# Sums of absolute differences on half an image of one sample, with the quantised images passed once through DRAM

## The chip, the cores and the metric

The kernel runs on one core of one Trainium2 chip. The metric is the time of that core for one execution, in microseconds (us). Runs that are compared are fast ones, within 1.5% of the fastest of their kernel. Where only a single run exists, it is unknown whether it was a fast one, and the text says "in one run".

In this text PE is TensorE, DVE is VectorE, ACT is ScalarE, POOL is GpSimd and SP is SyncE. SP computes nothing here: it issues most of the transfers.

## The reference, cut to what matters

The network has four layers and an encoder and decoder on 16 samples of 32 channels of 128 x 128. Only the second layer (`_L1_conv`) is changed in earnest. It quantises the normalised image to whole numbers from -127 to 127, and for each of 32 filters sums |patch - weight| over 32 channels and 9 taps.

```python
def _ste_quant(x, scale):                  # value only
    return round(clip(x / scale, -127, 127))

def _adder2d(qx, qw):
    """out[n,f,i,j] = -sum_{c,kh,kw} |patch - w|"""
    patches = conv_general_dilated_patches(qx, (3, 3), (1, 1), [(1, 1), (1, 1)])
    ...
    def per_out(wk):
        return -sum(abs(pr - wk[None, :, None]), axis=1)

qx = _ste_quant(x, INPUT_SCALE)            # INPUT_SCALE = 2 ** -7
qw = _ste_quant(weight, s_w)               # s_w: a power of two from max |weight|
ys = _adder2d(qx, qw) * INPUT_SCALE
```

## The kernel before

The identity used is |q - w| = 2 max(q - w, 0) - q + w. DVE or ACT makes a **tile** d = max(q - w, 0) for one tap: in this kernel for one filter and four samples, in the changed one for four filters and one sample. PE multiplies the tile by a matrix of -1/64 that sums the channels into the output rows of PSUM. The term in q needs the same matmuls for every filter ("corrections", with 1/128), and the term in w is a constant (`sumw`).

In this form the 128 partitions are (channel, four samples), and a chunk is 32 rows of four samples. There are 16 chunks.

```python
R = 32
with tc.tile_pool(name="s1_ps", bufs=8, space=PSUM) as ps:
    for g in range(NG):                      # four groups of four samples
        for ch in range(H // R):             # four chunks of 32 rows
            xc = xp.tile([128, R + 2, W], F32, name="xc")
            nc.sync.dma_start(xc[:, off : off + n, :], cb_view(x1, g, lo, n))
            ...                              # quantise into qb; qa is its copy with borders
            nc.scalar.copy(qa[:, off : off + n, 1 : W + 1], qv)
            acc = [ps.tile([128, 512], F32, name="acc") for _ in range(8)]
            for tap in range(9):             # corrections: 288 matmuls
                for k in range(8):
                    for j in range(4):
                        nc.tensor.matmul(acc[k][32 * j : 32 * j + 32, :], sel16[:, 8, :],
                                         window(tap)[:, 4 * k : 4 * k + 4, :],
                                         start=tap == 0, stop=False)
            for f8 in range(8):
                for tap in range(9):
                    for j in range(4):       # j == 3 on ACT (2 buffers), others on DVE (6)
                        ...
                        nc.vector.tensor_scalar(d, window(tap), qw[:, i : i + 1], 0.0,
                                                ALU.subtract, ALU.max)
                    ...                      # 32 matmuls add the four tiles to acc
            for k in range(8):               # finishing
                nc.vector.scalar_tensor_tensor(v, acc[k], sumw, v, ALU.subtract, ALU.add)
                nc.vector.bn_stats(stat[:, g, 8 * ch + k, :], v)
            nc.scalar.dma_start(cb_view(x2, g, R * ch, R), xc[:, 1 : R + 1, :])
```

All eight buffers of the pool in PSUM (the banks, below) belong to one chunk, so the next chunk's corrections cannot begin before the last tile of this one: the last matmuls of the second chunk's tiles start at 1978.59 us, the corrections of the third at 1998.43.

Of the kernel before, what the change touches and what calls it, by code (L numbers as in the profile page):

```python
# [6 lines left out]
F32 = mybir.dt.float32  # L7
F16 = mybir.dt.float16
# [7 lines left out]
HW = H * W  # L16
CHW = C * HW
NG = 4
# [20 lines left out]
def cb_view(t, g, row0, nrows):  # L39

    return bass.AP(t.tensor, t.offset + g * 4 * CHW + row0 * W, [[HW, C], [CHW, 4], [1, nrows * W]])


# [28 lines left out]
def norm_stats(nc, pool, ps, mv, n, avg, eps):  # L72



    mean = pool.tile([128, n], F32, name="ns_mean")
    nc.vector.tensor_copy(mean, mv[:, :, 0])
    p1 = ps.tile([128, 512], F32, name="ps")
    nc.tensor.matmul(p1[:, :n], avg, mean, start=True, stop=True)
    m = pool.tile([128, n], F32, name="ns_m")  # L80
    nc.vector.tensor_copy(m, p1[:, :n])
    d = pool.tile([128, n], F32, name="ns_d")
    nc.vector.tensor_sub(d, mean, m)
    nc.vector.tensor_mul(d, d, d)
    nc.vector.tensor_add(d, d, mv[:, :, 1])
    p2 = ps.tile([128, 512], F32, name="ps")
    nc.tensor.matmul(p2[:, :n], avg, d, start=True, stop=True)
    v = pool.tile([128, n], F32, name="ns_v")
    nc.vector.tensor_copy(v, p2[:, :n])
    return m, inv_sqrt(nc, pool, v, n, eps)  # L90
# [10 lines left out]
def stage0(nc, tc, keep, cst, x, w0, b1, b2, x1):  # L101
# [3 lines left out]
    with ExitStack() as ctx:  # L105
# [104 lines left out]
        with tc.tile_pool(name="s0_ps2", bufs=2, space=PSUM) as ps:  # L210
            out = []
            for v in norm_stats(nc, sm, ps, mv, NG, cst["avg2_bc"], 1e-5):
                p = ps.tile([128, 512], F32, name="ps")
                nc.tensor.matmul(p[:, :NG], cst["bc_to_cb"], v, start=True, stop=True)
                out.append(keep.tile([128, NG], F32, name=f"s0_out{len(out)}"))
                nc.vector.tensor_copy(out[-1], p[:, :NG])
            return out


def stage1(nc, tc, keep, cst, sel16, m1, r1, x1, w, x2):  # L220
# [4 lines left out]
    R = 32  # L225
    with ExitStack() as ctx:
        sm = ctx.enter_context(tc.tile_pool(name="s1_sm", bufs=1))
        r128 = sm.tile([128, NG], F32, name="r128")
        nc.vector.tensor_scalar(r128, r1, 128.0, None, ALU.mult)


        qw = sm.tile([128, 288], F32, name="qw")
        nc.sync.dma_start(qw, bass.AP(w.tensor, w.offset, [[288, 32], [0, 4], [1, 288]]))
        top = sm.tile([128, 1], F32, name="top")
        nc.vector.tensor_reduce(top, qw, AX.X, ALU.max, apply_absolute_value=True)
        alltop = sm.tile([128, 1], F32, name="alltop")
        nc.gpsimd.partition_all_reduce(alltop, top, 128, bass_isa.ReduceOp.max)
        scale = sm.tile([128, 1], F32, name="scale")
        nc.vector.tensor_scalar(scale, alltop, 1.0 / 127.0, 1e-8, ALU.mult, ALU.max)
        nc.vector.tensor_scalar(scale, scale, 2.0**0.5, None, ALU.mult)  # L240
        nc.vector.tensor_scalar(scale.bitcast(I32), scale.bitcast(I32), 0x7F800000, None, ALU.bitwise_and)
        nc.vector.reciprocal(scale, scale)
        nc.vector.tensor_scalar(qw, qw, scale, -127.0, ALU.mult, ALU.max)
        nc.vector.tensor_scalar(qw, qw, 127.0, RND, ALU.min, ALU.add)
        nc.vector.tensor_scalar(qw, qw, RND, None, ALU.subtract)
        neg = sm.tile([128, 288], F32, name="neg")
        nc.vector.tensor_scalar(neg, qw, -1.0, None, ALU.mult)


        taps = sm.tile([128, 32], F32, name="taps")  # L250
        nc.vector.tensor_reduce(taps, qw.rearrange("p (f t) -> p f t", t=9), AX.X, ALU.add)
        tapb = sm.tile([128, 32, 4], F32, name="tapb")
        nc.vector.tensor_tensor(tapb, bcast(taps[:, :], 2, 4), bcast(cst["m4_cb"], 1, 32), ALU.mult)
        sumw = sm.tile([128, 1], F32, name="sumw")
        with tc.tile_pool(name="s1_ps0", bufs=1, space=PSUM) as ps:
            p = ps.tile([128, 512], F32, name="ps")
            nc.tensor.matmul(p[:, :1], tapb.rearrange("p f b -> p (f b)"), cst["ones"][:, :1], start=True, stop=True)
            nc.vector.tensor_scalar(sumw, p[:, :1], 2.0**-7, None, ALU.mult)

        stat = sm.tile([128, NG, 32, 6], F32, name="stat2")  # L260
        xp = ctx.enter_context(tc.tile_pool(name="s1_x", bufs=2))
        tp = ctx.enter_context(tc.tile_pool(name="s1_t", bufs=1))
        qp = ctx.enter_context(tc.tile_pool(name="s1_q", bufs=2))
        dp = ctx.enter_context(tc.tile_pool(name="s1_d", bufs=2))
        with tc.tile_pool(name="s1_ps", bufs=8, space=PSUM) as ps:
            for g in range(NG):
                for ch in range(H // R):
                    lo, hi = max(R * ch - 1, 0), min(R * ch + R + 1, H)
                    off = lo - (R * ch - 1)
                    n = hi - lo  # L270
                    xc = xp.tile([128, R + 2, W], F32, name="xc")
                    nc.sync.dma_start(xc[:, off : off + n, :], cb_view(x1, g, lo, n))


                    qa = qp.tile([128, R + 2, W + 2], F16, name="qa")
                    qb = qp.tile([128, R + 2, W], F16, name="qb")
                    t = tp.tile([128, R + 2, W], F32, name="t")
                    tv, qv = t[:, off : off + n, :], qb[:, off : off + n, :]
                    nc.vector.tensor_scalar(
                        tv, xc[:, off : off + n, :], m1[:, g : g + 1], r128[:, g : g + 1], ALU.subtract, ALU.mult  # L280
                    )
                    nc.vector.tensor_scalar(tv, tv, -127.0, 127.0, ALU.max, ALU.min)
                    nc.vector.tensor_scalar(qv, tv, RND, RND, ALU.add, ALU.subtract)
                    nc.scalar.copy(qa[:, off : off + n, 1 : W + 1], qv)
                    nc.gpsimd.memset(qa[:, :, 0], 0.0)
                    nc.gpsimd.memset(qa[:, :, W + 1], 0.0)
                    for edge, row in ((ch == 0, 0), (ch == H // R - 1, R + 1)):
                        if edge:
                            nc.gpsimd.memset(qa[:, row, :], 0.0)
                            nc.gpsimd.memset(qb[:, row, :], 0.0)  # L290

                    def window(tap):
                        kh, kw = tap // 3, tap % 3
                        return qb[:, kh : kh + R, :] if kw == 1 else qa[:, kh : kh + R, kw : kw + W]

                    acc = [ps.tile([128, 512], F32, name="acc") for _ in range(8)]
                    for tap in range(9):
                        for k in range(8):
                            for j in range(4):
                                nc.tensor.matmul(  # L300
                                    acc[k][32 * j : 32 * j + 32, :],
                                    sel16[:, 8, :],
                                    window(tap)[:, 4 * k : 4 * k + 4, :],
                                    start=tap == 0,
                                    stop=False,
                                )
                    for f8 in range(8):
                        for tap in range(9):
                            ds = []
                            for j in range(4):  # L310
                                i = 9 * (8 * j + f8) + tap
                                if j == 3:
                                    d = dp.tile([128, R, W], F16, name="d_act", bufs=2)
                                    nc.scalar.activation(d, window(tap), AF.Relu, bias=neg[:, i : i + 1])  # L314
                                else:
                                    d = dp.tile([128, R, W], F16, name="d_dve", bufs=6)
                                    nc.vector.tensor_scalar(  # L317
                                        d, window(tap), qw[:, i : i + 1], 0.0, ALU.subtract, ALU.max
                                    )
                                ds.append(d)  # L320
                            for k in range(8):
                                for j in range(4):
                                    nc.tensor.matmul(  # L323
                                        acc[k][32 * j : 32 * j + 32, :],
                                        sel16[:, f8, :],
                                        ds[j][:, 4 * k : 4 * k + 4, :],
                                        start=False,
                                        stop=f8 == 7 and tap == 8,
                                    )
                    for k in range(8):  # L330
# [830 lines left out]
```

## Time and profile before

| | before |
|---|---|
| time, median of 3 runs | 9255.92 us (9252.01 to 9258.56) |
| PE busy | 7875.1 us, 85% of the span |
| DVE busy | 6114.6 us, 66% |
| ACT busy | 5084.6 us, 55% |
| first and last DVE tile of the changed layer start at | 1432.0 us and 5943.0 us |

One more view of this kernel beside those that the prediction shows is the busy time of the engines in a stretch inside the layer. Its columns are: stretch, length, busy us (and instructions) of PE, PE's weight loads, DVE, ACT and POOL, granted clock (the share of full speed that the chip granted to PE), DMA share (the busy share of the 16 DMA engines), GB/s.

```profile
1520.00:5550.00 4030.00, 3852.39 (x36850) 1952.10 (x36850) 3926.91 (x3347) 3746.84 (x1040) 66.30 (x42) 0.99 0.04 16
```

DVE is busy for 97% of it, and the DMA engines stand nearly idle, at a share of 0.04.

### The profile page before, as it was taken

The page shows a single profiled execution, that of the slowest core. Times are in us where ns is not written, and L with a number is a line of the kernel's source. Part 1 is how long each engine was busy: PE and PEld are TensorE (multiplying, and loading weights), DVE is VectorE, ACT ScalarE, POOL GpSimd, SP SyncE. Part 2 cuts the span into 40 slices and gives each one's busy share as a digit, 9 for nine tenths or more (in the row PEclk, how much of TensorE's full clock was granted, in tenths as well). Part 3 has the DMA queues.
Part 4 walks back from the last instruction along what each step waited for, and adds up shares of the span by engine and source line. Part 5 has one row for each costly group of instructions (what it writes and reads, how often), then busy time and mean ns, then how long its engine had stood idle before and what let it go on. Part 6 is the DMA issues. An engine that isn't in the chain of part 4 may idle for free.

```text
span 9251.5 us, 253991 instructions
## 1 busy us (share of the span) xinstructions
PE 7875.1 (85%) x117746; PEld 5052.1 (55%) x117746; DVE 6114.6 (66%) x7543; ACT 5084.6 (55%) x3270; POOL 332.4 (4%) x529
## 2 busy tenths in 40 slices
PE   4999988999999999999999999794845968768955
PEld 3888874445444444544445544493734645545832
DVE  5444448999999999999999999830634233232233
ACT  1444437989989899998989989700000110101122
POOL 0111110000000000000000000000000000000000
PEclk9999998999999999999999999855555968778977
DMA  9799921000000000000000000242731111111067
GB/s 199 57 80 78 73 28 30 20 20 20 1 20 20 20 20 12 10 20 20 20 20 1 20 20 10 74 126 54 253 107 53 42 57 36 52 42 36 26 161 182
DMA packets 1503138, 494.74 MB, mean 53 GB/s; under 512 B 1416956, under 2 KB 1420540, under 8 KB 1486332
## 3 DMA queue, kind: packets, MB, share of 16 engines
q1 hardware_dynamic: 1460764, 365.54, 24.5%
q10 hardware_dynamic: 41312, 112.95, 3.7%
q8 instruction: 922, 15.11, 0.7%
q14 instruction: 140, 1.15, 0.0%
HBM read 331.12 MB, written 147.33 MB: 52 GB/s over the span
## 4 chain that ended last, share of the span: by engine, by line
DVE 41%; PE 38%; issue 15%; DMA 2%; SPq 2%; ACT 1%; DVEq 0%; ACTq 0%; POOL 0%; POOLq 0%
DVE d_dve L317 35%; PE acc L905 10%; PE pg L179 5%; PE pg L180 4%; PE acc L646 4%; PE acc L565 3%; PE pg L181 2%; PE acc L300 2%; PE p L379 2%; PE acc L793 2%; PE pf L479 1%; DVE xc L332 1%; PE acc L323 1%; DVE stat L333 1%; PE pa L459 1%
## 5 line engine op out<-in xcount | busy, mean ns | idle before, releaser
L323 PE MATMUL acc<-d_dve,sel 128*32 128x512 f16 x27648 | 3994.7, 379 | 43.7 <-DVE d_dve L317 43.3
L323 PEld LDWEIGHTS <-sel 128*32 128x32 f16 x36864 | 2057.5, 95 | 2042.1 <-issue 217.6
L314 ACT ACTIVATE d_act<-qa,neg 128x4096 f16<-128x4096 f16 x768 | 2803.3, 3697 | 131.4 <-PE acc L323 130.3
L317 DVE TENSOR_SCALAR d_dve<-qa,qw 128x4096 f16<-128x4096 f16 x2304 | 2788.5, 1279 | 110.6 <-PE acc L323 86.0
L323 PE MATMUL acc<-d_act,sel 128*32 128x512 f16 x9216 | 2181.2, 380 | 0.0
L314 ACT ACTIVATE d_act<-qb,neg 128x4096 f16<-128x4096 f16 x384 | 1419.4, 3696 | 0.0
L317 DVE TENSOR_SCALAR d_dve<-qb,qw 128x4096 f16<-128x4096 f16 x1152 | 1409.5, 1279 | 0.0
L905 PE MATMUL acc<-xp,fo_all 32*32 32x512 f32 x25600 | 934.9, 625 | 55.4 <-DVE pooled L806 48.8
L905 PEld LDWEIGHTS acc<-xp,fo_all 32*32 32x32 f32 x25600 | 658.4, 105 | 321.6 <-issue 161.6
L179 PE MATMUL pg<-h,bd 128*128 128x256 f32 x2048 | 652.2, 401 | 58.7 <-DVE h L199 58.4
L190 ACT ACTIVATE gt<-pg,bias 128x256 f32<-128x256 f32 x1024 | 400.9, 474 | 546.0 <-PE pg L181 545.8
L180 PE MATMUL pg<-h,bd 128*128 128x256 f32 x2048 | 622.8, 386 | 0.0
L817 ACT ACTIVATE y<-pooled,fo_b 32x128 f32<-32x128 f32 x256 | 102.4, 400 | 843.6 <-DVE pooled L806 840.2
L646 PE MATMUL acc<-xp 32*32 32x108 f32 x16384 | 326.1, 376 | 233.4 <-issue 228.3
L933 DVE TENSOR_TENSOR acc<-acc,cut 128x4 f32<-128x4 f32 x256 | 28.8, 166 | 700.4 <-PE acc L905 699.3
L181 PE MATMUL pg<-xn,bd 128*128 128x2 f32 (+62 forms) x2048 | 425.8, 289 | 9.4 <-DVE xn L163 9.4
L181 PEld LDWEIGHTS pg<-xn,bd 128*128 128x128 f32 x2048 | 396.6, 194 | 66.4 <-DVE xn L163 10.2
L180 PEld LDWEIGHTS pg<-h,bd 128*128 128x128 f32 x2048 | 398.2, 194 | 56.9
L646 PEld LDWEIGHTS acc<-xp 32*32 32x32 f32 x16384 | 257.3, 135 | 302.4 <-issue 282.6
L617 DVE TENSOR_SCALAR xp<-xp,stats 128x2560 f32<-128x2560 f32 (+1 forms) x64 | 101.0, 1579 | 461.5 <-DMA xp<-x_d 461.4
L194 DVE TENSOR_TENSOR c<-c,gt 128x256 f32<-128x256 f32 x256 | 108.4, 424 | 450.0 <-ACT gt L190 450.0
L179 PEld LDWEIGHTS pg<-h,bd 128*128 128x128 f32 x2048 | 341.4, 195 | 65.6 <-issue 50.0
(233 smaller groups left out, 5197.9 us busy)
## 6 DMA issues: line engine op xcount, KB each, us to landing
xr<-x_d SPq DMA_DIRECT2D x64, 1024.0 KB
xp<-x_d SPq DMA_DIRECT2D x48, 1280.0 KB
x_in<-in_x_dram SPq DMA_DIRECT2D x16, 2048.0 KB
res<-in_x_dram SPq DMA_DIRECT2D x32, 1024.0 KB
x_d<-res SPq DMA_DIRECT2D x32, 1024.0 KB
x_d<-xc ACTq DMA_DIRECT2D x16, 2048.0 KB
x_d<-xr ACTq DMA_DIRECT2D x32, 1024.0 KB
out_dram<-xr ACTq DMA_DIRECT2D x32, 1024.0 KB
```

The source lines that it names most:

```text
L179: nc.tensor.matmul(pg[:, q], wmat(0, q), h_in[:, :, 1:], start=True, stop=False)
L180: nc.tensor.matmul(pg[:, q], wmat(1, q), h_in[:, :, :H], start=False, stop=False)
L181: nc.tensor.matmul(pg[:, q, :, : t + 1], wmat(2, q), xn[:, 2 * c : 2 * c + 2, j, : t + 1], start=False, stop=True,)
L190: nc.scalar.activation(gt[:, q], pg[:, q], AF.Tanh if q == 3 else AF.Sigmoid, bias=bias[:, q : q + 1])
L300: nc.tensor.matmul(acc[k][32 * j : 32 * j + 32, :], sel16[:, 8, :], window(tap)[:, 4 * k : 4 * k + 4, :], start=tap == 0, stop=False,)
L314: nc.scalar.activation(d, window(tap), AF.Relu, bias=neg[:, i : i + 1])
L317: nc.vector.tensor_scalar(d, window(tap), qw[:, i : i + 1], 0.0, ALU.subtract, ALU.max)
L323: nc.tensor.matmul(acc[k][32 * j : 32 * j + 32, :], sel16[:, f8, :], ds[j][:, 4 * k : 4 * k + 4, :], start=False, stop=f8 == 7 and tap == 8,)
L379: nc.tensor.matmul(p1[:, i, :], xh[:, 16 * half + i, :], cst["cas"], start=True, stop=True)
L565: nc.tensor.matmul(acc[blk][32 * j : 32 * j + 32, : rows * n], self.w[part, par, tap, :], src[part, top : top + rows, left : left + n], st ...
L646: nc.tensor.matmul(gram[blk][32 * j : 32 * j + 32, at : at + 36 * n], xp[rows, l, 2 + 32 * j : 34 + 32 * j], xp[rows, l : l + n, 32 * j : ...
L905: nc.tensor.matmul(acc[blk][32 * j : 32 * j + 32, :], wf["all"][rows, tap, :], xp[rows, 4 * j + kh : 4 * j + kh + 4, kw : kw + W], start=t ...
```

## The change

The intent is fewer and longer DVE and ACT instructions, and a boundary between pieces of work that costs DVE nothing. A piece is now a half: 64 rows of one sample. There are 32 halves, each of 72 tiles of 8192 or 8320 values, 54 on DVE and 18 on ACT. The 128 partitions are (four filters, channel), so the same quantised channel must lie in four groups of 32 partitions. To get it there, each image is quantised once, stored in DRAM as float16 with borders (`q_d`), and loaded back four-fold (`q`). A half needs four PSUM banks. Finishing of a half is written after the eighth tile of the next one, and quantising of the next sample after the 21st.

The core of the diff (statistics in the new layout, constants and weight layout are cut):

```diff
-    R = 32
+    R = 64
+    P = W + 2
...
+def jc_rows(t, b, half, n=16 * W):
+    return bass.AP(t.tensor, t.offset + b * CHW + half * 64 * W, [[16 * W, 4], [HW, C], [1, n]])
...
+        def quantise(b, half):
+            t = xp.tile([128, 16 * W], F32, name="xq")
+            nc.sync.dma_start(t, jc_rows(x1, b, half))
+            nc.scalar.activation(t, t, AF.Identity, bias=shift[:, b : b + 1], scale=r128[:, b : b + 1])
+            qt = ring[half]
+            ...                                        # DVE: round and clip to qt
+            nc.sync.dma_start(
+                bass.AP(q_d.tensor, first, [[16 * P, 4], [(H + 2) * P, C], [1, 16 * P]]), flat)
+        def finish(b, half, acc):
+            xr = rp.tile([128, 16 * W], F32, name="xr1")
+            nc.sync.dma_start(xr, jc_rows(x1, b, half))
+            ...                                        # DVE: four pairs on 512 columns
+            nc.sync.dma_start(jc_rows(x2, b, half), xr)
...
-            for g in range(NG):
-                for ch in range(H // R):
+        for b in range(B):
+            for half in range(2):
+                q = qp.tile([128, R + 2, P], F16, name="q")                # 2 buffers
+                nc.sync.dma_start(
+                    q, bass.AP(q_d.tensor, first, [[0, 4], [(H + 2) * P, C], [1, (R + 2) * P]]))
+                acc = [ps.tile([128, 512], F32, name="acc") for _ in range(4)]
+                for tap in range(9):                                       # corrections: 144
+                    for j in range(4):
+                        for k in range(4):
+                            nc.tensor.matmul(acc[k][32 * j : 32 * j + 32, :], sel16[rows, 8, :],
+                                             q[rows, row : row + 4, kw : kw + W],
+                                             start=tap == 0, stop=False)
+                for i in range(72):
+                    d = dp.tile([128, R, P], F16, name="d_act" if act else "d_dve",
+                                bufs=2 if act else 4)
+                    ...                                # i % 4 == 3 on ACT, others on DVE
+                    ...                                # 16 matmuls add the tile to acc
+                    if i == 7 and before:
+                        finish(*before)
+                    if i == 20 and b + 1 < B:
+                        quantise(b + 1, half)
+                before = b, half, acc
+        finish(*before)
```

## The prediction

> **What bounds the kernel now.** I read the page's slices first, to find which stretch the change touches:
>
> ```profile
> PE   4999988999999999999999999794845968768955
> DVE  5444448999999999999999999830634233232233
> ACT  1444437989989899998989989700000110101122
> PEclk9999998999999999999999999855555968778977
> ```
>
> Only the second layer (the sums of absolute differences) is edited in earnest. It is the plateau from the 7th to the 26th slice (231 us each), where three engines look full. PE is the one not to believe: the groups by shape tell why.
>
> ```profile
> L323 PE MATMUL acc<-d_dve,sel 128*32 128x512 f16 x27648 | 3994.7, 379 | 43.7 <-DVE d_dve L317 43.3
> L314 ACT ACTIVATE d_act<-qa,neg 128x4096 f16<-128x4096 f16 x768 | 2803.3, 3697 | 131.4 <-PE acc L323 130.3
> L317 DVE TENSOR_SCALAR d_dve<-qa,qw 128x4096 f16<-128x4096 f16 x2304 | 2788.5, 1279 | 110.6 <-PE acc L323 86.0 <-ACT qa L284 24.6
> L317 DVE TENSOR_SCALAR d_dve<-qb,qw 128x4096 f16<-128x4096 f16 x1152 | 1409.5, 1279 | 0.0
> L284 ACT COPY qa<-qb 128x4224 f16<-128x4224 f16 x8 | 29.7, 3718 | 128.2 <-DVE qb L283 128.2
> L332 DVE SCALAR_TENSOR_TENSOR xc<-acc,sumw,xc 128x512 f32<-128x512 f32 x128 | 89.0, 735 | 2.0 <-PE acc L323 2.0
> L333 DVE BATCH_NORM_STATS2 stat<-xc 128x6 f32<-128x512 f32 x128 | 81.4, 676 | 0.0
> ```
>
> A matmul's 379 ns are latency; where all operands are ready, the timeline shows four starting every 0.21 us, so a round (3 DVE tiles, 1 ACT tile, 32 matmuls) needs 8 x 0.21 = 1.7 us of PE. The makers of tiles are slower. The timeline around the start of the third chunk:
>
> ```profile
> 1969.70 3.67 DVE L317 TENSOR_SCALAR d_dve<-qb,qw 128x4096 f16<-128x4096 f16 x3
> 1973.29 3.67 DVE L317 TENSOR_SCALAR d_dve<-qa,qw 128x4096 f16<-128x4096 f16 x3
> 1976.88 2.54 DVE L279 TENSOR_SCALAR t<-xc,s_out,r 128x4352 f32<-128x4352 f32 x1
> ...
> 1992.12 2.40 DVE L283 TENSOR_SCALAR qb<-t 128x4352 f16<-128x4352 f32 x1
> 1994.56 3.82 ACT L284 COPY qa<-qb 128x4352 f16<-128x4352 f16 x1 [16.46 <-DVE qb L283]
> ...
> 1998.43 3.60 PE L300 MATMUL acc<-qa,sel 128*32 128x512 f16 x32 [18.39 <-ACT qa L284]
> ...
> 2018.02 7.26 DVE L317 TENSOR_SCALAR d_dve<-qa,qw 128x4096 f16<-128x4096 f16 x6 [3.25 <-PE acc L323]
> ...
> 2018.42 7.31 ACT L314 ACTIVATE d_act<-qa,neg 128x4096 f16<-128x4096 f16 x2
> ```
>
> Two readings. Inside a chunk, three DVE tiles start every 3.59 us (1969.70 to 1973.29) and ACT tiles follow each other at 7.31 - 3.70 = 3.61 us: both engines are at the bound. 72 rounds at 3.60 are 259 us. Between chunks, finishing, quantising and the copy on ACT stand one after another: PE idles 18.4 us, then 288 correction matmuls (L300) take until 2015.8 before the first tile is used, and DVE waits again on full buffers. The chain of waits gives the chunk starts 1430.80, 1713.88, 1998.43, 2281.08: 284 us a chunk, so about 24 us of 284 are the boundary.
>
> [...] the tile takes 1279 ns, and tiles follow at 1.197 us[...] (qa, pitch 130, equals qb, 1279 ns); a strided destination is not shown here. [...] this kernel's f16 matmuls show only four at once.
>
> **The change part by part.** A chunk of 32 rows of four samples becomes two halves (64 rows of one sample). The difference arithmetic stays the same, in half as many instructions of twice the length. Per half:
>
> - *DVE tiles:* 54 (i not 3 mod 4). 36 of 8192 values: [...] 2.263 us. 18 with kw = 1 take the whole pitch, 8320 values: [...] 2.297 us. Sum 81.5 + 41.3 = 122.8 us. Two halves save 216 x 1.197 - 245.6 = 13 us per old chunk.
> - *Quantising:* DVE loses L279, L282 and L283 with halo rows (7.4 us per chunk) and gets two ops on 2048 values[...]. 1.9 us per half.
> - *Finishing:* 4 x (L332 + L333). Two pairs take 2.51 us in the timeline, so 5.0 us per half; it moves to the eighth tile of the next half.
> - DVE in all: 122.8 + 1.9 + 5.0 = **129.8 us a half**.
> - *ACT:* 18 tiles, [...] 126.9; the copy (3.8 us a chunk) goes, an affine op on 2048 values comes, 1.9. **128.8 us a half.**
> - *PE:* 72 x 16 matmuls at 0.053 us = 61 us, hidden. The 144 corrections now use 32-row, 32-column tiles on the unreplicated rows: at the L905 group's pace (25600 in about 1.0 ms, 40 ns) 6 us, an estimate; DVE's four buffers cover 9 us. With four banks a half and eight in all, the next half need not wait for the finishing.
> - *DMA:* the quantised half out (0.53 MB) and back four-fold (2.2 MB), and x1 twice: 16 us every 130 at the 250 GB/s of the first xc load (2.1 MB, 1411.4 to 1419.7). Hidden.
> - *Start:* in the instruction order of the changed kernel all four quantisings of samples 0 and 1 stand before DVE's first tile. Loads of 5 MB, stores of 1 MB and the first 2.2 MB back[...]: first tile at 1411 + 42 = 1453 us, where it is 1432 now: +21.
> - *End:* the last finishing is 4 pairs, not 8: -5. Stage 2's smaller setup lies beside the 41.6 us load of xh.
>
> The two engines come out within 1 us of each other, coupled by four and two buffers through one in-order PE. DVE falls back 7 us at its lumps and regains 7.05 - 6.82 = 0.23 us a round; the buffers hold 9 us, so most is absorbed. I choose 1 us of coupling per half: 130.8. Last DVE tile at 1453 + 32 x 130.8 = 5639, less 5 because the first half has nothing to finish: 5634, where it is 5944 now. -310 - 5 gives 9256 - 315 = 8941; with a little less coupling 8920. I put **8935 us**, 3.5% less.
>
> **The rivals.** *A strided destination or the 2-byte offset at PE costs extra.* [...] For it: nothing in this trace writes such rows. Against: strided reads cost nothing[...]. A PE at half pace for kw = 1 tiles would still fit (81 of 130 us). *Coupling:* DVE waits for ACT's affine op, or both for buffers, 4 us a half: 9040. For it: the equality of the two sums and bufs=2 on ACT. Against: in the instruction order most affine ops stand well ahead of DVE's use. *The round trip through DRAM is not hidden:* q's load sits behind stores on one queue. Stores and loads are issued by tile 21 of 72, leaving 90 us; 15 us a half if wrong, 9400. *The boundary was mostly hidden already*, so that only the instruction saving counts: 16 x 13 = 208 less, 9050. Against: the 18.4 us PE wait and the 284 us period.
>
> **The range.** The sums without any coupling give about 8905; 2 us more coupling a half give 9000. I take **8875 to 9010**. Faster by over 2% needs under 9071, 4 us a half more than predicted: **0.88**. Within 2%: **0.07**. Slower: **0.05**[...].
>
> **What would show it.** DVE tiles near 2345 ns (2263 plus the 82 ns overlap) in both forms and ACT tiles near 7105 ns; chunk starts 131 us apart; DVE and ACT both at 97% or more inside a half; corrections under 6 us a half; first tile near 1453. Wrong if the row-wise tiles take 4 us, if DVE's idle before L354 is over 130 us in all with PE as the releaser, if waits on q's DMA recur each half, or if the granted clock in the stage falls below 0.9.

Its times for the new instructions and for the loads at the start are estimates: the profile before has DVE tiles of one length only (4096 values, 1279 ns) and ACT tiles of one length (4096 values, 3697 ns), and no tile that is written in rows.

## The result, and the profile after

| | before | after |
|---|---|---|
| time, median of 4 runs | 9255.11 us (9252.01 to 9258.56) | 9934.66 us (9932.76 to 9937.02) |
| ratio of fast runs | 1 | 1.0734, interval 1.0716 to 1.0753 |
| first DVE tile of the layer starts at | 1432.0 us | 1509.7 us |
| last DVE tile of the layer starts at | 5943.0 us | 6649.6 us |

The changed kernel is 7.3% slower, where 3.5% faster was predicted. A ratio here and below is the mean time of one kernel's fast runs over that of the other's fast runs of the same rounds, so it is not quite the ratio of the medians quoted beside it. The outputs are correct.

The page's slices after the change, the same rows as the prediction shows of before (the span in 40 equal slices, busy share in tenths):

```profile
PE   4999954545454455445544555559465686859965
...
DVE  5444426978797778777877787783153323332233
ACT  1444326978797778777877787770000010101122
...
PEclk9999977978788888778877888885555786868977
```

DVE and ACT were the engines at the bound, at 8 to 9 tenths. Now they stand at 7 to 8, and the plateau is longer. PE fell to 4 or 5, as intended. So something else holds DVE and ACT. The groups by shape say how much and what released them (busy us, mean ns of one; then the idle time just before, and what ended most of it):

```profile
L354 DVE TENSOR_SCALAR d_dve<-q,qw 128x8192 f16<-128x8192 f16 x1152 | 2661.9, 2348 | 65.7 <-PE acc L359 41.9 <-DMA q<-q_d 22.8
L354 DVE TENSOR_SCALAR d_dve<-q,qw 128x8320 f16<-128x8320 f16 x576 | 1372.0, 2382 | 958.4 <-PE acc L359 958.2
L352 ACT ACTIVATE d_act<-q,neg 128x8192 f16<-128x8192 f16 x384 | 2714.9, 7114 | 632.0 <-PE acc L359 607.2 <-DMA q<-q_d 24.8
L336 PE MATMUL acc<-q,sel 32*32 32x512 f16 x4608 | 155.7, 472 | 1173.0 <-DMA q<-q_d 1173.0
```

A DVE tile takes 2348 or 2382 ns and an ACT tile 7114 ns, as predicted (2345, 7105). What was not predicted is the idle time: 958.2 + 41.9 = 1000.1 us in which DVE waits for PE to give a buffer back, while PE's corrections (L336) wait 1173.0 us for the load of `q`. The account closes: from the first tile at 1509.7 to the end of the last (it starts at 6649.6 and ends about 6652) are 5142 us; less 1001 idle, 4141 us are left as DVE's work, and 32 x 129.8 - 5 = 4149 had been predicted.

The waits of the layer (1450 to 6600 us; columns: waited for, us in total, times, longest us):

```profile
PE acc L336 <- DMA q<-q_d: 1173.0, 32, 92.0
DVE d_dve L354 <- PE acc L359: 1000.1, 62, 46.4
ACT d_act L352 <- PE acc L359: 870.3, 32, 46.7
```

The corrections waited 32 times, once for each half. To see how a wait of PE's for `q` stops DVE, take one sample. PE's timeline around the start of a wait:

```profile
2677.04 1.06 PE L359 MATMUL acc<-d_dve,sel 128*32 128x512 f16 x16 [0.39 <-DVE d_dve L354]
2727.73 0.65 PE L336 MATMUL acc<-q,sel 32*32 32x512 f16 x15 [49.63 <-DMA q<-q_d]
2728.31 1.90 PE L359 MATMUL acc<-d_dve,sel 128*32 128x512 f16 x16
```

The same stretch on DVE:

```profile
2665.49 20.54 DVE L354 TENSOR_SCALAR d_dve<-q,qw 128x8320 f16<-128x8320 f16 x9
2730.26 77.53 DVE L354 TENSOR_SCALAR d_dve<-q,qw 128x8320 f16<-128x8320 f16 x34 [44.23 <-PE acc L359]
...
2840.85 13.74 DVE L354 TENSOR_SCALAR d_dve<-q,qw 128x8320 f16<-128x8320 f16 x6 [18.97 <-PE acc L359]
```

And the chain of waits over it, in order of time (start, us, what):

```profile
2665.60 22.28 DMA q_d<-qt
2687.95 39.73 DMA q<-q_d
...
2797.33 39.14 DMA q<-q_d
```

PE takes its instructions in their order: it stands still for 49.63 us before the corrections at 2727.73, and the matmuls of tiles behind them start at 2728.31. Right behind the matmuls of one tile stand corrections of the **next** half, and they need `q` of the next half. That `q` is loaded only after the quantised rows were stored, 22.28 + 39.73 us. Tiles of the current half that are ready stand behind and cannot be consumed. DVE fills its four buffers, ACT its two, and both stop, here for 44.23 and 45.50 us.

Halves are counted from 0, so the even ones are the first half of a sample and the odd ones the second. The 44.23 us lie in an odd half and are a wait for the `q` of the even half that follows. The 18.97 us lie in that even half and are a wait for the `q` of the next odd half, whose load starts only when a `q` buffer comes free, at 2797.33. Over the layer DVE's timeline has 14 stalls of the first kind, of 32 to 46 us (590 us in all), and 17 that begin where the corrections stand early in a half, of 19 to 31 us (359 us in all). Together they are 949 of the 1000.1 us; the rest are short ones.

Where PE's corrections stand was readable before any run. This is the order of the instructions on PE, not a profile (the trace of the run has the same places):

```
before: corrections of every chunk: one block, ahead of the chunk's first tile
after:  corrections of half 1: within half 0, from behind tile 9 to tile 27
        corrections of half 2: within half 1, tile 7 to 22
        corrections of half 3: within half 2, tile 7 to 18
        corrections of half 4: within half 3, tile 29 to 46
        corrections of half 5: within half 4, tile 7 to 17
```

The scheduler could move them forward because four of the eight PSUM banks are now free for the next half. In the kernel before, the full banks kept them in place (e7 tests this: DVE's wait for PE is 78.8 us there).

**Why is the load so slow?** It moves 2.196 MB (128 partitions of 66 x 130 values of two bytes) in 39.73 us, which is 55 GB/s. The prediction took 250 GB/s from the first `xc` load of the kernel before. The busy times in the stretch of this load, and in the one after it (columns as above):

```profile
2688.00:2728.00 40.00, 0.27 (x15) 0.14 (x15) 0.00 (x0) 0.20 (x1) 0.00 (x0) 0.50 0.23 55
2728.00:2797.30 69.30, 49.93 (x816) 21.01 (x802) 67.02 (x30) 63.60 (x10) 0.00 (x0) 0.92 0.01 2
```

During the load the DMA share is 0.23. The access pattern's outermost count is 4 (`[[0, 4], ...]`); that of `xc` was 32 (`[[HW, C], ...]`). The `xc` load moved 2.16 MB in 8.32 us, in a stretch with a share of 0.97 (348 GB/s with all that moved beside it). That the count makes the difference is at this point the reading; e3 and e4 show the time of the split load. All five transfers of the layer have this shape: `xq`, `xr`, the store to `q_d`, `q` and the store of x2. Several of them at once had no larger share: from 1475 to 1505 us, with two loads of `q` and two stores to `q_d` issued, the share was 0.25 (87 GB/s).

### The profile page after: what moved, and what is told of

The parts are those of the page before. It is cut to its first block, busy times and chain, and to the rows that moved or that the text cites. A ratio compares the mean times of both kernels' runs of the same rounds, so it can differ in the third digit from the quotient of the medians.

```text
span 9934.3 us, 249580 instructions
## 1 busy us (share of the span) xinstructions
PE 6213.4 (63%) x117740; PEld 4017.6 (40%) x117740; DVE 5854.6 (59%) x5842; ACT 5005.8 (50%) x2710; POOL 268.7 (3%) x483
## 4 chain that ended last, share of the span: by engine, by line
PE 35%; issue 26%; DMA 19%; DVE 11%; ACT 7%; SPq 1%; ACTq 0%; POOL 0%; DVEq 0%; POOLq 0%
DMA q<-q_d 13%; PE acc L941 9%; ACT d_act L352 7%; DVE d_dve L354 5%; PE pg L174 4%; PE pg L175 4%; PE acc L682 3%; DMA q_d<-qt 3%; PE pg L176 2%; PE acc L601 2%; PE acc L359 2%; PE p L415 2%; DMA xq<-x_d 2%; PE acc L829 1%; PE pf L515 1%
## 5 line engine op out<-in xcount | busy, mean ns | idle before, releaser
L354 DVE TENSOR_SCALAR d_dve<-q,qw 128x8192 f16<-128x8192 f16 (+1 forms) x1728 | 3944.0, 2360 | 1024.2 <-PE acc L359 1000.1
L352 ACT ACTIVATE d_act<-q,neg 128x8192 f16<-128x8192 f16 (+1 forms) x576 | 4068.1, 7149 | 895.1 <-PE acc L359 870.3
L359 PE MATMUL acc<-d_dve,sel 128*32 128x512 f16 x27648 | 1973.1, 417 | 766.5 <-DVE d_dve L354 763.9
L359 PEld LDWEIGHTS <-sel 128*32 128x32 f16 x36864 | 1118.6, 103 | 2767.2 <-issue 2143.9
L359 PE MATMUL acc<-d_act,sel 128*32 128x512 f16 x9216 | 696.7, 427 | 624.9 <-ACT d_act L352 624.3
L336 PE MATMUL acc<-q,sel 32*32 32x512 f16 x4608 | 155.7, 472 | 1173.0 <-DMA q<-q_d 1173.0
L336 PEld LDWEIGHTS <-sel 32*32 32x32 f16 x4608 | 49.5, 91 | 1302.1 <-DMA q<-q_d 764.5
```

The source lines that it names most:

```text
L336: nc.tensor.matmul(acc[k][32 * j : 32 * j + 32, :], sel16[rows, 8, :], q[rows, row : row + 4, kw : kw + W], start=tap == 0, stop=False,)
L352: nc.scalar.activation(dst, src, AF.Relu, bias=neg[:, i : i + 1])
L354: nc.vector.tensor_scalar(dst, src, qw[:, i : i + 1], 0.0, ALU.subtract, ALU.max)
L359: nc.tensor.matmul(acc[k][32 * j : 32 * j + 32, :], sel16[:, f8, :], d[:, row : row + 4, c : c + W], start=False, stop=i == 71,)
```

## The experiments

The theory that the experiments test is this: **slow transfers** (outermost count 4) land late, and **instructions that wait for them in an in-order engine's stream** (the corrections on PE) turn each late landing into a stall of DVE and ACT. Rivals: the round trip itself is too long for the time it has, wherever the instructions stand; or the granted clock, which fell to 0.82 in the layer from 0.99, slows PE and with it the others. All kernels compute the correct result. "After" is the changed kernel, from which every diff starts. The kernel before took 9252.41 us in the job of e1, e2, e3 and e5, 9259.61 in that of e4 and e6, 9241.2 (one run) beside e7, and 9253.66 and 9253.70 in those of e8 and of e9 and e10.

### e1: corrections held behind the half before

The context manager (an "edge" below) tells the scheduler only where the instructions stand; it adds no wait.

```diff
+                with tc.issue_after(last.ins) if last else ExitStack():
                     for tap in range(9):          # corrections
...
-                            nc.tensor.matmul(     # of the tiles
+                            last = nc.tensor.matmul(
```

> One edit: the corrections of a half are pinned on PE behind the last matmul of the half before; all else as in the changed kernel. Theory A (PE's order: the corrections of the next half stand among the tiles of this one and wait there for q, and the tiles behind them wait with them): DVE's idle before L354 falls from 1024 us to under 150, the wait of the corrections for q from 1173 us to under 150, and the time is near 8935 us plus the 57 us that the start lost, 8990 (8930 to 9060). Theory B (the round trip through DRAM itself is too slow, whatever the order): q's wait moves to DVE and ACT, and the time stays above 9700. Theory C (a slower tensor clock, 0.79 in the mean, slows the tiles): the clock stays low with short idle gaps, and the time stays above 9700.

Measured: 8965.61 us (8959.25 to 8974.88, 4 runs), ratio to before 0.9685 (0.9671 to 0.9700). The waits of the layer:

```profile
PE acc L337 <- DMA q<-q_d: 91.1, 1, 91.1
...
ACT xq L296 <- DMA xq<-x_d: 80.1, 4, 36.6
...
DVE d_dve L355 <- PE acc L360: 36.4, 5, 33.9
```

The wait for `q` is left once, at the start, and DVE's 1000.1 us are 36.4. No transfer was made faster: in the chain at the start `xq`, the store to `q_d` and `q` took 26.71, 26.05 and 37.01 us (27.82, 26.03 and 36.84 in the changed kernel). But one caution: the scheduler also moved the quantising on DVE, from tile 16 or 17 to tile 4 with both halves in one place, and with it the order of the transfers. So this is not a change on PE alone; e8 was made to part the two.

### e2: only the load of q split

```diff
-                nc.sync.dma_start(
-                    q, bass.AP(q_d.tensor, first, [[0, 4], [(H + 2) * P, C], [1, (R + 2) * P]]))
+                for j in range(4):
+                    nc.sync.dma_start(q[32 * j : 32 * j + 32],
+                        bass.AP(q_d.tensor, first, [[(H + 2) * P, C], [1, (R + 2) * P]]))
```

> One edit: each load of q is four transfers of 32 partitions, so the outermost count is 32 in place of 4; PE's order stays as it was (corrections at tile 7 and tile 29). If the outermost count of 4 is what makes a load slow, it falls from 40 us to about 10 at near 220 GB/s. Theory A then: the odd halves' wait (19 us of DVE) goes, the even halves' (44 us) shrinks by 30 to about 15, DVE's idle is 200 to 400 us, the time 9150 to 9350 us. Theory B: the same direction, so this run sizes the part of the rate and does not part A from B. If the loads stay at 40 us, the outermost count isn't the reason.

Measured: 9128.26 us (9126.24 to 9132.94, 4 runs), ratio 0.9859 (0.9843 to 0.9876), slightly below the expected range. The corrections' waits for `q` fell from 1173.0 us to 282.6. The waits of the layer:

```profile
PE acc L338 <- DMA q<-q_d: 282.6, 21, 80.6
...
DVE d_dve L356 <- PE acc L361: 186.5, 68, 13.0
```

The instructions may still stand in the wrong place; with this one load faster, DVE waits 186.5 us instead of 1000.1. The other four transfers are not split: in the chain at the start `xq` took 27.44 us and the store to `q_d` 26.02 (27.82 and 26.03 in the changed kernel).

### e3: both at once, all five transfers split

The split is that of e2, done for all five: four transfers of 32 partitions with the channel outermost.

```diff
-def jc_rows(t, b, half, n=16 * W):
-    return bass.AP(..., t.offset + b * CHW + half * 64 * W, [[16 * W, 4], [HW, C], [1, n]])
+def jc_rows(t, b, half, j, n=16 * W):
+    return bass.AP(..., t.offset + b * CHW + (half * 64 + 16 * j) * W, [[HW, C], [1, n]])
...
+            for j in range(4):                    # xq; likewise xr and the store of x2
+                nc.sync.dma_start(t[32 * j : 32 * j + 32], jc_rows(x1, b, half, j))
...
+            for j in range(4):
+                nc.sync.dma_start(
+                    bass.AP(q_d.tensor, first + 16 * P * j, [[(H + 2) * P, C], [1, 16 * P]]),
+                    flat[32 * j : 32 * j + 32])
```

> The pin, and all five transfers of the stage (x1 for quantising and for finishing, the quantised store, q, x2) as four of 32 partitions. Theory A: about the same plateau as the pin alone (the transfers are hidden then), and a start earlier by 40 to 60 us: first tile near 1455 in place of 1510, time 8900 to 8980 us, and 30 to 80 us under the pin alone. Theory B: far below the pin alone, by over 300 us.

Measured: **8873.94 us** (8871.68 to 8877.62, 4 runs), ratio 0.9586 (0.9572 to 0.9600). This is the lowest time and beats both kernels. The stretch of 1520 to 5550 us, here and then in the changed kernel:

```profile
1520.00:5550.00 4030.00, 2556.29 (x40336) 1165.09 (x40336) 4030.00 (x1997) 4015.40 (x591) 0.00 (x0) 0.91 0.20 44
```

```profile
1520.00:5550.00 4030.00, 2074.87 (x32171) 904.80 (x32171) 3214.45 (x1579) 3198.88 (x472) 0.00 (x0) 0.82 0.13 37
```

DVE is busy for all of the 4030 us at a granted clock of 0.91. So a clock below the 0.99 of before costs nothing here, because PE has over a third of its time left (2556 of 4030 us busy). In the changed kernel PE was busy for only half of the stretch, and its clock was low where it idled: 0.50 during the load shown above, 0.92 in the 69 us after it. The low clock went with the stalls and did not make them: that rival is refuted. The first pair of DVE's finishing in two halves that follow each other:

```profile
3014.28 1.39 DVE L319 SCALAR_TENSOR_TENSOR xr<-acc,sumw,xr 128x512 f32<-128x512 f32 x2
...
3143.82 1.39 DVE L319 SCALAR_TENSOR_TENSOR xr<-acc,sumw,xr 128x512 f32<-128x512 f32 x2
```

The period is 3143.82 - 3014.28 = 129.5 us. The prediction's sum for DVE was 129.8.

### e4: all five split, the order left to the scheduler

The split of e3 without the edge of e1. The corrections now stand from tile 7 (odd halves) and tile 33 (even halves) of the half before, where the changed kernel has them from tile 7 and tile 29.

> All five transfers of the stage as four of 32 partitions, without the pin: PE's order has the corrections of the next half at tile 7 (odd halves) and tile 33 (even halves) of this one. Theory A says that the order costs only where q lands after PE comes to that place. Worked out from the runs before: quantising ends about 46 us into a half, store and load then take some 14 us, so q lands near 60 us, and tile 33 is 33 x 1.8 = 60 us into the half; in the odd halves the load of some 10 us is over by tile 7 (13 us). So next to no wait: 8870 to 8930 us, within 50 us of the pin with the split (8874). If the order alone cost much, whatever the transfers, it would be above 9000.

Measured: 8884.08 us (8879.42 to 8891.72, 4 runs), ratio 0.9597 (0.9581 to 0.9613), as expected. It is the same arithmetic with nearly the same order as the changed kernel, and 1050.6 us less. The chain at the start of the layer:

```profile
1442.32 12.30 DMA q<-q_d
1454.75 2.41 DVE d_dve L361 x2
```

The four parts of `q` land within 12.30 us of the issue of the last of them (13.6 of the first), where the one transfer took 36.84 in this place and 39.73 later. While they are in flight, with other transfers beside them, the DMA share is 0.95, instead of 0.23:

```profile
1442.40:1454.40 12.00, 7.23 (x96) 3.44 (x101) 0.00 (x0) 0.00 (x0) 0.00 (x0) 0.50 0.95 201
```

Taken over the share that is about 212 GB/s (201 / 0.95), and about 239 before (55 / 0.23): between these two stretches the share differs about fourfold, the rate taken over it by 12%. The first tile starts at 1454.75 (predicted 1453), 55 us earlier than in the changed kernel; 55 + 1000 is about the gain. With fast transfers, holding the corrections in place shows no gain: the 10 us between e3 and e4 are 0.1%, less than the executions of one kernel differ by (0.14% in e4). So the slow transfers are necessary for the loss.

### e5: a third buffer for q

```diff
-        qp = ctx.enter_context(tc.tile_pool(name="s1_q", bufs=2))
+        qp = ctx.enter_context(tc.tile_pool(name="s1_q", bufs=3))
```

> One edit: three buffers for q in place of two; PE's order is nearly the same. Theory A: the odd halves' loads no longer wait for a buffer to come free, so their 19 us of DVE's idle times 16 go (about 300 us), the even halves' 44 us stay because they wait for the quantised store and the load: about 9630 us. If the buffer wasn't the cause in the odd halves: 9900.

Measured: 9567.38 us in one run, 367 us less than the changed kernel, a little better than expected. The corrections' waits for `q` fell from 32 to 16. On DVE's timeline the 14 long stalls stay (32 to 49 us, 594 us in all), and the 17 short ones are gone. DVE's wait for PE is 632.9 us in place of 1000.1, and the 367 us between them are the whole gain. So the waits for the `q` of the odd halves came from the load waiting for a free buffer. The expectation fell short by some 60 us mostly because it reckoned 16 stalls of 19 us.

### e6: corrections placed on purpose at one tile

All transfers slow; corrections of the next half held behind tile 36 of the half before (they stand at tiles 37 to 54). DVE's order is as in the changed kernel. This is a dose: late enough that less of the load is left to wait for, too early to have none.

```diff
+                    if i == 36:
+                        mark = mm                  # the last matmul of tile 36
...
+                last = mark                        # corrections issue after last
```

> A dose: slow transfers as in the changed kernel, the corrections pinned behind tile 36 of the half before (they stand from tile 37 to 54). Theory A: in the changed kernel q of an even half lands 108 us after DVE began the half before; PE came to it at tile 29 (52 us) and DVE idled 44 us, 12 us less than the 56 between. At tile 37 (66.5 us) that is 108 - 66.5 - 12 = 30 us, times 16 = 480 us over the pin at the half's end (8966): 9440 us (9370 to 9510). The odd halves, whose q lands after 40 us, pay nothing. A theory without the place in the order has no reason for a time between 8966 and 9935.

Measured: 9555.28 us in one run, a miss by 45 us above the range. The direction is right, 379 us less than the changed kernel, and the stall for the `q` of an even half was as expected:

```profile
3204.19 63.74 DVE L355 TENSOR_SCALAR d_dve<-q,qw 128x8192 f16<-128x8192 f16 x28 [29.47 <-PE acc L360]
```

But a wait that the theory did not have was large in this run: the affine op of the quantising (L296), which stands between ACT's tiles, waited 327.3 us for `xq`. In the changed kernel it had waited 187.4 us. From 3632 us on DVE has a second stall of 20 to 28 us in most pairs of halves, which the theory did not have; the one that ends at 5201.96, for example, follows a wait of 27.80 us of that op. That led to e8 and e9.

### e7: four PSUM banks

With half the banks, a half fills the pool again, as a chunk did in the kernel before. Finishing must then stand at the end of its own half.

```diff
-        ps = ctx.enter_context(tc.tile_pool(name="s1_ps", bufs=8, space=PSUM))
+        ps = ctx.enter_context(tc.tile_pool(name="s1_ps", bufs=4, space=PSUM))
...
-                    if i == 7 and before:
-                        finish(*before)
+                    if i == 71:
+                        finish(b, half, acc)
```

> Where the freedom came from: slow transfers as in the changed kernel and no pin, but the accumulators have four PSUM banks in place of eight and the finishing stands at the end of its own half. The corrections of the next half must then wait for the banks, and in PE's order they stand behind the last tile of the half, as in the kernel before (whose chunk filled all eight banks). Theory A: the waits of tiles for q go as with the pin (8966); what comes in their place is 2 to 4 us a half in which DVE waits for the last matmuls before it can finish: 9030 to 9100 us. If the order isn't the cause, it is slower than the changed kernel (9935), since it overlaps less.

Measured: 8990.25 us in one run, better than expected. DVE's wait for PE is 78.8 us in all, with slow transfers and without any edge. Taking the free banks away puts the corrections back behind the last tile and removes the loss. But the finishing stands elsewhere, and as in e1 the scheduler also moved the quantising (to DVE's tile 4), so this run shows where the freedom came from and not what the place of the corrections alone is worth.

### e8: the edge of e1, with DVE's order kept as in the changed kernel

```diff
+                        made = nc.vector.tensor_scalar(dst, src, ...)
...
                     if i == 7 and before:
-                        finish(*before)
+                        with tc.issue_after(made.ins):
+                            finish(*before)
                     if i == 20 and b + 1 < B:
-                        quantise(b + 1, half)
+                        with tc.issue_after(made.ins):
+                            quantise(b + 1, half)
```

DVE's and SP's orders are those of the changed kernel from half 3 on. The corrections are held as in e1, the transfers slow.

> In the run with the pin alone the scheduler had also moved the quantising on DVE (from the 17th tile to the 5th of a half, both halves' in one place), so that q landed earlier: a second difference. Here finishing and quantising are held on DVE behind the tiles where the changed kernel has them, and from the third half on the orders on DVE and of the transfers are the changed kernel's; only the place of the corrections on PE differs (slow transfers, corrections behind the last tile). Theory A: q of an even half lands about 106 us into the half before, PE comes to the corrections at 129 us, so nothing waits: 8965 us (8930 to 9010), DVE's idle before its tiles under 120 us. If the earlier quantising was what helped in that run, the even halves' 44 us come back in part: over 9250 us.

Measured: 9405.34 us (9398.0 to 9417.25, 4 runs), ratio 1.0163 (1.0146 to 1.0180). This is a clear miss by 440 us. The waits of the layer:

```profile
PE acc L360 <- ACT d_act L353: 1252.8, 346, 32.9
...
ACT xq L296 <- DMA xq<-x_d: 534.9, 30, 33.1
DVE d_dve L355 <- PE acc L360: 460.9, 123, 28.6
...
PE acc L337 <- DMA q<-q_d: 92.2, 1, 92.2
```

The edge did what it should: PE's wait for `q` is left once, at the start. But a second instruction now does on ACT what the corrections did on PE. The affine op stands in ACT's stream and waits for `xq`; ACT's tiles behind it are late, PE waits for them in order (1252.8 us, where it was 624.3 in the changed kernel), and DVE's buffers fill. So e1 owes a part of its speed to what the scheduler had moved beside the corrections.

### e9: e8 with only x's transfers split

`q` and the store to `q_d` stay slow; only `xq`, `xr` and the store of x2 are split as in e3. If ACT's wait is the cause of e8's loss, this alone should remove it.

> The run before (e8) took PE's waits for q away (92 us are left, all at the start) and still came to 9405 us, 440 over what was expected. Its trace names a second wait of the same kind: ACT's affine op for quantising stands between ACT's tiles and waits for the x1 rows, 535 us in 30 waits, since their load is issued late and takes 28 us. Here the order is that of e8, and only the three transfers of x1 and x2 are four of 32 partitions; the quantised store and q stay slow. If the late x1 rows are the second wait, ACT's wait for xq falls under 60 us and the time to 8930 (8890 to 8980). If slow q transfers still cost something with the corrections at the end, it stays above 9100.

Measured: 8920.38 us (8911.86 to 8922.61, 4 runs), ratio 0.9636 (0.9620 to 0.9652), within the expected range and 485 us less than e8. The affine op now waits for `xq` once, at the start of the layer, instead of 30 times and 534.9 us:

```profile
ACT xq L297 <- DMA xq<-x_d: 13.8, 1, 13.8
```

`q` is not split here. With its corrections behind the last tile it costs only at the start: DVE waits for it once, 51.2 us, where it was 16.4 in e3; these 35 us are most of the 46 us between the two.

### e10: e8's order with all five split

> e8's orders with all five transfers split: both waits gone and the start early. The same as the pin with the split (8874) within 20 us if the place of the quantising on DVE matters for nothing once the transfers are fast; DVE then works through the stage at 129.5 us a half.

Measured: 8884.44 us (8883.53 to 8894.11, 4 runs), ratio 0.9602 (0.9588 to 0.9617), as expected. The same order took 521 us more with slow transfers (e8), and with fast ones it is within 11 us of e3.

### What the runs show together

| | after | e1 | e3 | e4 | e8 | e9 | e10 |
|---|---|---|---|---|---|---|---|
| corrections behind the last tile | no | yes | yes | no | yes | yes | yes |
| quantising where the changed kernel has it | yes | no | from half 6 on | nearly | yes | yes | yes |
| `q`, `q_d` split | no | no | yes | yes | no | no | yes |
| `xq`, `xr`, x2 split | no | no | yes | yes | no | yes | yes |
| time, us | 9934.66 | 8965.61 | 8873.94 | 8884.08 | 9405.34 | 8920.38 | 8884.44 |

Every version with all five transfers fast is within 11 us of the best, which is no clear difference. With slow ones the time is anything from 8966 to 9935, by where the waiting instructions stand. Three things stay open: what the slow transfers of x1 and x2 alone cost in the changed kernel's order (no run splits only these there), why e6's affine op waited so much more than the changed kernel's, and how much of e1's gain over e8 is from the place of the quantising and how much from the order of the transfers that came with it.

## Why the prediction was wrong

- **The failing step is the DMA bullet**: "16 us every 130 at the 250 GB/s of the first xc load (2.1 MB, 1411.4 to 1419.7). Hidden." The rate was taken from a transfer with an outermost count of 32 and used for transfers with 4. The load of `q` ran at 55 GB/s, 39.73 us instead of about 9, and the store before it took 22.28 us for 0.53 MB instead of about 2 (other transfers moved bytes beside it: share 0.23, 83 GB/s in all). Split, the load took about 12 us (12.30 in e4, 12.90 in e3, from the last issue). The sum itself was also low: 0.53 + 2.2 + 2 x 1.05 MB at 250 GB/s are 19 us, and the store of x2 is not in it.
- **"Hidden" was a second error in the same bullet.** It compared the length of a transfer with the time left until the half begins. What counted is the first instruction in PE's order that waits for it (1173.0 us of the corrections' waits). The prediction speaks of the order of quantisings, affine ops, stores and loads, but not of PE's, where the corrections stood 26 to 65 tiles early (from tile 7 to tile 46 of 72). The DMA engines as a whole were not short: their share was 0.13 in the stretch from 1520 to 5550 us.
- **"With four banks a half and eight in all, the next half need not wait for the finishing"** is true. It is also what let the scheduler move the corrections forward (e7). The prediction saw only the gain.
- **The rival "The round trip through DRAM is not hidden"** named the right place and gave 15 us a half, 9400. Measured: 1000.1 / 32 = 31 us a half, and 57 us at the start (1509.7 against 1453). It said that 90 us were left; `q`'s real need was 62 us after the quantising, which fits into 90, but the corrections did not wait until then. Its reading that the loads are issued by tile 21 does not hold in time. The load for an even half went out after the store, at 2687.95, some 68 us into the half before it. The load for an odd half went out when a `q` buffer came free, at 2797.33, some 3 us into the half before it, and met corrections at tile 7.
- **The start**, "first tile at 1411 + 42 = 1453": 1509.7, by the same slow transfers (27.82, 26.03 and 36.84 us in a row in the chain). With all five split, 1454.75 (e4).
- **The arithmetic was right.** DVE's tiles 2348 and 2382 ns (2345 predicted), ACT's 7114 (7105): with twice the values, 1.84 times the 1279 ns and 1.92 times the 3697 ns of before; 129.5 us a half in e3 (129.8). Corrections: in e8, where they stand in one block, the 144 at 3122.34 took 4.07 us, not 6. DVE's row-wise tiles (2348 ns) are no slower than the others, and the 16 matmuls of a tile take about 1.05 us in most places, so neither the destination in rows nor the offset of two bytes shows a cost: that rival is refuted.
- **Coupling of 1 us a half** did not show: in e3 the period is DVE's own sum. About 32 us of the 61 between 8935 and e3's 8874 are this term. Some 23 more are the end: from the start of the last tile to the end of the kernel e3 takes 3280.9 us, 27.6 less than the 3308.5 of before, and 5 had been predicted.
- **Its own signs** were well chosen: three of the four that should show it wrong came true (DVE idle over 130 us with PE as releaser, waits on `q` in each half, the clock below 0.9), and the fourth (row-wise tiles at 4 us) did not. The clock was the harmless one (e3: 0.91 and DVE full; e4 with nearly the changed kernel's order: 0.92).

## What to carry to other kernels

Before calling a transfer hidden, look at the outermost count of both access patterns and take the rate from a transfer of the same shape. Here a load of `q` with an outermost count of 4 took 39.73 us at 55 GB/s; four transfers of 32 partitions, with the channel outermost, brought the same bytes 12.30 us after the last issue. Then find, on each engine, the first instruction that waits for the transfer: free banks let the scheduler put PE's corrections 26 to 65 tiles ahead of where their result is needed, and the tiles behind them paid, 1000.1 us of DVE's time. With fast transfers the order hardly mattered here (within 11 us); with slow ones the times lay up to 970 us apart.
